# Sums of a graph-attention layer issued for two tiles at a time instead of three, a wait split over two accumulators, and four small operations given an earlier turn

## The chip, the cores and the metric

The kernel runs on one core of a Trainium2 chip. The metric is the device time of one execution in microseconds (us); of several runs the median is taken. A core has several engines, each of which works through its own list of instructions in order: TensorE (PE in the profile; PEld is its loading of weights) for matrix products and transposes, VectorE (DVE), ScalarE (ACT) and GpSimd (POOL) for elementwise work, and SyncE (SP), which here issues the transfers between memory and the core. [...]PE writes to PSUM, a small memory of accumulators, from which ACT or DVE must copy the results away ("evacuate" them) before the accumulator can be used again.

## The reference

The input is a graph with N = 3327 nodes, 256 features each, and a dense 3327 x 3327 matrix of edge weights, most of them zero. There are two layers, each of the form x = x + layer(relu(layernorm(x))).

Layer 0 runs two steps. In each, A is a sparsified attention matrix: logits q k^T over all pairs of nodes, softmax by row, and of each row the largest probabilities that together reach 0.9. R is the edge matrix plus identity, divided by its row sums.

```
for n in range(2):
    A  = top_p_attention(Xa, W1, W2, W3)      # 3327 x 3327
    Xf = R @ Xf
    Xa = A @ Xa
    Z  = Z + Xf @ U1[n].T + Xa @ U2[n].T
h = layernorm(X + Z) * g + b
```

Layer 1 is graph attention with four heads of 64 features:

```
e    = leaky_relu(s[:, :, None] + d[:, None, :], 0.2)   # per head, source i, neighbour j
e    = where(adj > 0, e, -inf)
attn = softmax(e over j)
out  = elu(attn @ hp)                                  # hp = h @ W, 64 features per head
```

The denominators of the last softmax are sums over j of the same exponentials that are multiplied with hp. They are the "sums" of this document.

## The kernel before

Nodes are split into 26 tiles of 128. The function that runs is `fast` (line 571).

**How the order comes about.** The kernel describes its work as pieces, each with an engine, an assumed length, a rank, the pieces it needs, and the buffers it takes and gives back (`put`). `Plan.order` (lines 470 to 567) then walks through an assumed time and gives each engine, whenever it is free, the piece of the lowest rank whose needs are met and whose buffers are free. The instructions are issued in exactly the order so found, so each engine's order is fixed in the program. A change of one rank or one buffer can therefore move pieces far away from it. The assumed lengths serve only to find the order; on the chip real durations count.

**Layer 0.** One row of the plan is a tile of 128 nodes against all 3327. There are 26 rows in each of two steps, 52 in all. For each row `search` (lines 1410 to 1458) finds the threshold above which probabilities are kept: logits on PE (L873), exponentials on ACT (L887), a first guess (`guess`, ACT), counts of what lies above the guess (`count`, ACT, L924, about 3.1 us each), a correction of the guess on POOL (`step`, lines 937 to 970), another count and step, in step 1 a third count with its step on DVE, then a search for the exact threshold on DVE (`window`, `sort`, `choose`) and the removal of everything below it (`drop`, L1034). `density` (lines 914 to 917) is four operations on one column of 128 values on ACT; its results are first read on POOL inside the first correction, that of L916 at L947 and that of L915 at L953. The first two counts of a row have rank -2.1 relative to the row, `density` -2.05: when both can go, the counts go first. `attention` (L1462) then transposes the row (PE L1047, copied by ACT L1052) and multiplies it with the features (PE L1059). `full` (L1477) holds the products of the edge matrix (PE L1091), which depend on no search and fill PE where a row isn't ready. At the end of a row small products and copies (L1227 to L1266) make the keys of the next step.

**Layer 1.** `attend_neighbours` (lines 1500 to 1811) goes over the 3327 target nodes in four quarters of W = 832 columns, and in each over 26 tiles of neighbours. Per tile:

- SP loads two blocks of the edge matrix, and ACT turns them into a mask of ones and zeros (L1623, L1624).
- DVE makes the exponentials times mask for four heads, two instructions of two heads each half (L1635), into an "e" buffer of the size 128 x 3328. The instructions' operand names vary: a tile uses one of four rotating buffers (pool "e") if its number modulo 7 is under 4, otherwise one of three fixed ones (shown as c and rhs in the profile; "e2" in the plan).
- PE multiplies the tile's features with the exponentials (L1651, `product`, two halves of two heads, each into its own accumulator of the PSUM pool "pl"; 8 records of the profile per half). One piece of the array is 128 x 64 there.
- PE adds the exponentials up over the neighbours (L1665, `sums`, 16 records per tile, in the accumulators acca and accf). One piece of the array is 128 x 32 there.

The sums of a tile are not issued with its products. They are gathered in a group of JG = 3 tiles, and each tile's sums give back its e buffer. After the last tile of a quarter, `leave` (lines 1707 to 1719) copies the two product accumulators (L1711, two instructions on ACT, one for each) and the sums (L1714) into one more buffer of the pool "e", called ot. From it, seven times, PE transposes 128 columns (L1732), DVE takes reciprocals (L1736), ACT makes the elu (L1744), DVE adds (L1748, L1749), and SP stores. This goes on while the next quarter's tiles already run. The last quarter ends with a different arrangement of the same work (lines 1767 to 1788).

The next quarter's first product needs both accumulators: it takes two "pl" buffers at once and needs the variable `evacuated`, the second of the two copies.

Of the kernel before, what the change touches and what calls it, by code (L numbers as in the profile page):

```python
# [10 lines left out]
F32 = mybir.dt.float32  # L11
# [8 lines left out]
P = 128  # L20
# [550 lines left out]
def fast(  # L571
# [59 lines left out]
    with ExitStack() as l0:  # L631
# [6 lines left out]
        ps_l = l0.enter_context(tc.tile_pool(name="ps_l", bufs=2, space=PSUM))  # L638
# [204 lines left out]
        plan = Plan(dict(rows=1, mvs=3, pl=2, px=2, acca=1, accf=1, accf0=1, accf1=1, et=3, at=4, y=1, e2=3, mask=2, **BUFS))  # L843
# [566 lines left out]
        def search(row, rank, keys, stats_of, fresh):  # L1410


            n, i = row.n, row.i
            got, a = [], None
            for g in range(2):

                def logits(g=g):
                    row.logits(2 * g)
                    row.logits(2 * g + 1)

                a = plan.put(
                    "PE", 2.1 - 0.7 * g, rank - 2.5, logits, needs=[keys, fresh, a], take=["pl", "pl"] + ["e", "sc"] * (1 - g)
                )
                for k in (2 * g, 2 * g + 1):
                    got.append(
                        plan.put("ACT", 1.15 if k < 3 else 0.5, rank - 2.5, row.exps, k, needs=[a], give=["pl"])
                    )
            row.pieces = dict(logits=a)
            a = plan.put("ACT", 0.35, rank - 2.4, row.row_sum, needs=[got])
            a = plan.put("POOL", 1.3, rank - 2.4, row.root, needs=[a, stats_of])  # L1430
            a = row.pieces["guess"] = plan.put("ACT", 1.0, rank - 2.4, row.guess, needs=[a])
            more = plan.put("ACT", 0.85, rank - 2.05, row.density, needs=[a])
            for j in range(2):
                got = [
                    plan.put("ACT", 3.05, rank - (2.1, 1.7)[j], row.count, j, fn, needs=[a])
                    for fn in (AF.Relu, AF.Sign)[j:]
                ]
                a = plan.put("POOL", (3.8, 4.7)[j], rank - (2.0, 1.6)[j], row.step, j, GP, needs=[got, more])
            if EVALS[n] == 3:
                a = row.pieces["counted"] = plan.put("ACT", 3.05, rank - 1.4, row.count, 2, AF.Sign, needs=[a])  # L1440
                a = plan.put("DVE", 2.7, rank - 1.3, row.step, 2, V, needs=[a])
            halves = []
            for h in range(2):
                for part in range(2):
                    a = plan.put(
                        "DVE", 3.2 - 2.0 * part, rank - 1.0, row.window, h, part, needs=[a], take=["y"] * (1 - part),
                        give=["y"] * part, lag=0.02, hold=1.95 * (1 - part),
                    )
                    halves.append(a)
            may = plan.put("POOL", 0.8, rank - 1.5, row.free, needs=[halves[2]])  # L1450
            a = plan.put("DVE", (1.8, 2.5)[n], rank - 1.0, row.sort, needs=[a])
            a = plan.put("DVE", 3.1, rank - 1.0, row.choose, needs=[a, may], take=["cum"])
            total = plan.put("POOL", 1.2, rank - 1.0, row.total, needs=[a], give=["cum"])
            drops = []
            for o in range(4):
                a = plan.put("DVE", 1.03, rank - 1.0, row.drop, o, needs=[a], hold=1.0)
                drops.append(a)
            return total, drops
# [41 lines left out]
        def attend_neighbours(rows, ends, done, fulls):  # L1500
# [1 line left out]

            W = NP // 4
            C = W // 2
            JG = 3
            logits_done = [r.pieces["logits"] for r in rows]
            freed = [p for p in done]
            extra = {}
# [23 lines left out]
            more = plan.put("SP", 0.02, 59.0, open_more, needs=[freed, opened], lag=0.0)  # L1532
# [41 lines left out]

            last, f_ = {}, None
            used_heads = [None, None]
            evacuated = None
            both = broadcast(0, 59.5)
            for b in range(4):
                lo = b * W  # L1580
                r0 = 60.0 + 10.0 * b
                q = {}
                tiles = range(lo // P, lo // P + 7)
                off = lo - tiles[0] * P

                def open_acc(q=q):
                    q["acc"] = [ps_l.tile([P, 2, 512], F32, name="pl") for _ in range(2)]

                def open_den(q=q):
                    q["den"] = [ps_a.tile([P, 512], F32, name=n) for n in ("acca", "accf")]  # L1590
# [1 line left out]
                seen, last_acc, last_den, last_e = [], None, None, None  # L1592
                group, groups_e = [], []
                for j in range(NT):
                    rank = r0 + 9.0 * j / NT
# [47 lines left out]

                    def product(a, j=j, held=held, q=q, open_acc=open_acc):

                        if j == 0 and a == 0:
                            open_acc()
                        for c in range(2):
                            for k in range(2):
                                h = 2 * a + k  # L1650
                                T.matmul(  # L1651
                                    q["acc"][a][k * FH : (k + 1) * FH, c, :C],
                                    main[:, j, h * FH : (h + 1) * FH],
                                    held["e"][:, h, c * C : (c + 1) * C],
                                    start=(j == 0),
                                    stop=(j == NT - 1),
                                )
# [20 lines left out]
                    else:  # L1678
# [6 lines left out]
                    x_ = plan.put(  # L1685
                        "DVE", 2.1, rank, exponents, 0, needs=[m_, both[0], ends[j][0], more if mine == "e2" else None,
                        logits_done, last_e], take=[mine], hold=2.0,
                    )
                    y_ = plan.put("DVE", 2.1, rank, exponents, 1, needs=[x_, both[1]], give=own, hold=2.0)
                    last_e = y_  # L1690
                    x_ = plan.put(
                        "PE", 1.42, rank, product, 0, needs=[x_, last_acc, evacuated], take=["pl", "pl"] * (j == 0)
                    )
                    last_acc = plan.put("PE", 1.42, rank, product, 1, needs=[x_, y_])
                    group.append((sums, mine))
                    if len(group) == JG or j == NT - 1:
                        for n_, (fn, name) in enumerate(group):
                            last_den = plan.put(
                                "PE", 1.42 + 0.2 * (n_ == 0), rank, fn, needs=[last_acc, last_den],
                                take=["acca", "accf"] * (j < JG and n_ == 0), give=[name],  # L1700
# [13 lines left out]
                            S.copy(q["ot"][:, 2, c], q["den"][c][:, :C])  # L1714

                r1 = r0 + 9.0
                evacuated = a = plan.put("ACT", 0.9, r1, leave, 0, needs=[last_acc], take=["e"], give=["pl"])
                evacuated = a = plan.put("ACT", 0.9, r1, leave, 1, needs=[a], give=["pl"])
                out_of = plan.put("ACT", 1.1, r1, leave, 2, needs=[a, last_den], give=["acca", "accf"])
                for x0 in range(0, W, P):  # L1720
                    m = min(P, W - x0, N - lo - x0)
# [74 lines left out]
                    elif x0 % (4 * P) == 0:  # L1796
                        f_ = plan.put("SP", 0.4, r1, fetch_all, needs=[used_heads[0] if x0 == 0 else [last_e, f_], touched], take=["e"] * (x0 > 0), lag=4.0)
                    a = plan.put(
                        "PE", 0.4, r1 + 0.02, turn, needs=[out_of], take=["px"], give=["e"] * (x0 + P >= W)
                    )  # L1800
                    if b == 3:
                        a = plan.put("DVE", 0.65, r1, quotient, needs=[a, f_], give=["px"])
# [27 lines left out]
        for n in range(STEPS):  # L1830
# [25 lines left out]
            if n == 0:  # L1856
# [25 lines left out]
                def layer1():  # L1882
# [8 lines left out]
                    give=["et", "et"],  # L1891
# [67 lines left out]
```

## Time and profile before

| | |
|---|---|
| three runs | 2218.48, 2219.33, 2220.72 us (median 2219.33) |
| profiled execution | 2222.8 us |
| its span | 2221.0 us |
| granted TensorE clock | 0.998 |
| PE busy | 2171.0 us in 11978 instructions |
| DVE, ACT, POOL busy | 1613.7, 1442.5, 931.3 us |
| L1651, products of layer 1, e buffers | 187.2 us, 1024 records of 515 ns |
| L1635, exponentials of layer 1, largest group | 128.6 us, 128 records of 1073 ns |
| L924, counts of layer 0 | 559.1 us, 182 records of 3072 ns |

In the rows of the profile an instruction is named by line, engine and operation, then what it writes and reads, with shapes; the numbers after it are the busy time of the group, the mean length of one in nanoseconds, and the idle time of the engine just before them with what ended it. Matrix products overlap in PE's pipeline, so the length of one record is longer than the pitch from one to the next. In a timeline, the first number is the start from the beginning of the span, the second the length of a run of equal instructions, and brackets give the idle time before it and what released it. Layer 1 takes about the last 480 us of the span; the quarters there begin some 119 us apart.

### The profile page before, as it was taken

Reading aid. Unit: us, or ns where it says so; the run is one execution under the profiler, and the core shown is the slowest. Engines: PE = TensorE matmul, PEld = TensorE weight load, DVE = VectorE, ACT = ScalarE, POOL = GpSimd, SP = SyncE. Lnnn points to the kernel's source line nnn. Section 1 sums busy time; section 2 is a strip of 40 time slices with the busy share of each in tenths; the row PEclk is TensorE's granted clock in tenths of the full one; section 3 lists DMA queues with packets and bytes.
Section 4 is the critical chain, followed back from the end, with each engine's and each line's share of the span. In section 5 each row is a group of like instructions: output and inputs, shape, how many; then the busy total and the mean of one; then the engine's idle time right before and its main releaser. Section 6 shows DMA issues by size and latency. Waiting matters only on the chain.

```text
span 2221.0 us, 35941 instructions
## 1 busy us (share of the span) xinstructions
PE 2171.0 (98%) x11978; PEld 1535.2 (69%) x11978; DVE 1613.7 (73%) x4229; ACT 1442.5 (65%) x2725; POOL 931.3 (42%) x2210
## 2 busy tenths in 40 slices
PE   7999999999999999999999999999999999999997
PEld 5388778777887788877878788887887433333333
DVE  5576656546655744277879877888777997989896
ACT  5766676567566661478888777878774455465553
POOL 5564455535544541256656666566653200000001
PEclk9999999999999999999999999999999999999999
DMA  4012121212212232622222222222225344444341
GB/s 120 1 45 80 52 71 54 71 52 62 71 54 71 71 91 67 189 82 60 63 58 63 62 72 74 80 62 64 67 77 152 117 130 143 116 137 126 107 127 50
DMA packets 192323, 183.75 MB, mean 83 GB/s; under 512 B 15386, under 2 KB 146176, under 8 KB 192128
## 3 DMA queue, kind: packets, MB, share of 16 engines
q1 hardware_dynamic: 190144, 180.10, 28.1%
q8 instruction: 96, 1.57, 0.3%
q10 hardware_dynamic: 1984, 1.26, 0.2%
q14 instruction: 99, 0.81, 0.1%
HBM read 164.41 MB, written 15.94 MB: 81 GB/s over the span
## 4 chain that ended last, share of the span: by engine, by line
PE 71%; issue 9%; ACT 8%; POOL 5%; DVE 5%; DMA 2%; SPq 0%; ACTq 0%; DVEq 0%; POOLq 0%
PE acca L1059 20%; PE accf L1091 20%; PE pl L1651 9%; PE pl L873 6%; ACT junk L924 6%; PE px L1047 6%; PE acca L1665 2%; PE accf L1665 2%; PE px L1258 2%; PE px L1209 1%; PE px L1354 1%; POOL sc L937 1%; ACT et L1052 1%; DVE e L1635 1%; PE px L1236 1%
## 5 line engine op out<-in xcount | busy, mean ns | idle before, releaser
L1059 PE MATMUL acca<-rhs,et 128*128 128x256 f32 x2704 | 620.7, 380 | 1.7 <-ACT et L1052 1.6
L924 ACT ACTIVATE junk<-e,sc 128x3327 fp8e5<-128x3327 f32 x182 | 559.1, 3072 | 48.0 <-POOL sc L969 46.6
L1059 PEld LDWEIGHTS acca<-rhs,et 128*128 128x128 f32 x2704 | 499.4, 191 | 66.0 <-ACT et L1052 4.8
L1091 PE MATMUL accf<-c,at 128*128 128x256 f32 x1352 | 313.5, 382 | 6.1 <-ACT f L1098 6.1
L1091 PE MATMUL accf<-main,at 128*128 128x257 f32 x1352 | 310.3, 381 | 3.0 <-DMA at<-in_adjt_dram 2.8
L979 DVE SCALAR_TENSOR_TENSOR y<-e,sc 128x1664 f32<-128x1664 f32 x104 | 208.1, 2001 | 127.1 <-POOL sc L966 125.1
L1052 ACT COPY et<-px 128x512 f32<-128x512 f32 (+1 forms) x364 | 192.6, 553 | 142.0 <-PE acca L1059 83.4
L1091 PEld LDWEIGHTS accf<-c,at 128*128 128x128 f32 x1352 | 250.0, 190 | 48.3 <-ACT f L1098 10.9
L1091 PEld LDWEIGHTS accf<-main,at 128*128 128x128 f32 x1352 | 251.0, 190 | 44.9 <-issue 6.5
L984 DVE MAX8 cands<-y 128x8 f32<-128x208 f32 x832 | 242.4, 361 | 3.6
L1034 DVE SCALAR_TENSOR_TENSOR e<-e,thr 128x832 f32<-128x832 f32 x208 | 212.9, 1079 | 2.0
L887 ACT ACTIVATE e<-pl 128x1024 f32<-128x1024 f32 x208 | 179.0, 863 | 37.6 <-PE pl L873 36.9
L1624 ACT ACTIVATE et<-at 128x448 bf16<-128x448 f32 (+1 forms) x204 | 112.3, 550 | 137.4 <-DVE e L1635 81.6
L1047 PE MATMUL px<-ident,e 128*128 128x128 f32 x1352 | 191.4, 274 | 7.1 <-ACT et L1052 2.3
L1784 POOL TENSOR_TENSOR qq<-qq 128x256 f32<-128x256 f32 x4 | 3.0, 755 | 453.7 <-ACT qq L1780 453.7
L1047 PEld LDWEIGHTS px<-ident,e 128*128 128x128 f32 x1352 | 160.1, 141 | 47.0 <-issue 11.8
L1651 PE MATMUL pl<-e,main 128*64 128x416 f32 x1024 | 187.2, 515 | 0.0
L873 PE MATMUL pl<-kt,qq 64*128 64x512 f32 (+1 forms) x832 | 173.5, 535 | 0.0
L1651 PEld LDWEIGHTS pl<-e,main 128*64 128x64 f32 x1024 | 71.1, 137 | 107.3 <-issue 91.9
L1635 DVE SCALAR_TENSOR_TENSOR e<-c,low,et 128x832 f32<-128x832 f32 x128 | 128.6, 1073 | 7.9 <-PE accf L1665 3.6
L873 PEld LDWEIGHTS pl<-kt,qq 64*128 64x128 f32 x832 | 71.6, 186 | 83.9 <-issue 77.9
L1635 DVE SCALAR_TENSOR_TENSOR e<-qq,low,et 128x832 f32<-128x832 f32 x120 | 120.4, 1076 | 2.6 <-ACT e L1711 2.0
(527 smaller groups left out, 3083.9 us busy)
## 6 DMA issues: line engine op xcount, KB each, us to landing
at<-in_adjt_dram SPq DMA_DIRECT2D x414, 256.0 KB
at<-in_adjt_dram SPq DMA_DIRECT2D x102, 192.0 KB
at<-in_adjt_dram SPq DMA_DIRECT2D x52, 128.0 KB
ys<-ystage SPq DMA_DIRECT2D x26, 256.0 KB
rhs<-in_x_dram SPq DMA_DIRECT2D x26, 128.0 KB
ystage<-in_x_dram SPq DMA_DIRECT2D x26, 128.0 KB
base<-ys SPq DMA_DIRECT2D x26, 128.0 KB
x1s<-ystage SPq DMA_DIRECT2D x26, 128.0 KB
```

The source lines that it names most:

```text
L873: T.matmul(pl[:, r, :m], qq[half, self.i, :], kt[half, 512 * k : 512 * k + m], start=True, stop=True,)
L887: S.activation(self.e[:, 1024 * k : 1024 * k + 2 * w].rearrange("p (r w) -> p r w", r=2), pl, AF.Exp, accum_out=(self.p0, self.p1, self.p2 ...
L924: S.activation(junk[:, :N], self.e[:, :N], fn, bias=t, scale=-1.0, accum_out=dst, saturate=False)
L979: V.scalar_tensor_tensor(self.y[:, : hi - lo], self.e[:, lo:hi], self.up, self.e[:, lo:hi], ALU.is_lt, ALU.mult, accum_out=(self.h0, self. ...
L984: V.max(self.cands[:, o // PIECE, :], self.y[:, o - lo : min(o + PIECE, hi) - lo])
L1034: V.scalar_tensor_tensor(piece, piece, self.thr[:, o : o + 1], piece, ALU.is_gt, ALU.mult)
L1047: T.transpose(pt[:, k, :], self.e[:, j * P : (j + 1) * P], ident)
L1052: S.copy(self.et[g][:, :m, :], self.pt.pop(g)[:, :m, :])
L1059: T.matmul(self.acc, et[:, j - 4 * g, :], rhs[self.n][:, j, :], start=(j == 0), stop=(j == NT - 1))
L1091: T.matmul(self.acc[:, : self.w], self.at[j // JC][:, j % JC, :], self.src[:, j, : self.w], start=(j == 0), stop=(j == NT - 1),)
L1635: V.scalar_tensor_tensor(held["e"][:, k, :], extra["both"][b % 2][:, k, :], low[:, j, k : k + 1], held["mask"], ALU.max, ALU.mult,)
L1651: T.matmul(q["acc"][a][k * FH : (k + 1) * FH, c, :C], main[:, j, h * FH : (h + 1) * FH], held["e"][:, h, c * C : (c + 1) * C], start=(j == 0),
```

## The change

Three edits. The size of a group of sums, JG, goes from 3 to 2. The two product accumulators of a quarter are opened one at a time: the first half product takes one "pl" buffer and waits for the first copy, the second half product takes the other and waits for the second copy. And `density` gets the rank -2.2, lower than that of the row's first two counts, so that the plan issues it ahead of them when both can go.

```diff
--- before.py
+++ after.py
@@ -1429,7 +1429,7 @@
             a = plan.put("ACT", 0.35, rank - 2.4, row.row_sum, needs=[got])
             a = plan.put("POOL", 1.3, rank - 2.4, row.root, needs=[a, stats_of])
             a = row.pieces["guess"] = plan.put("ACT", 1.0, rank - 2.4, row.guess, needs=[a])
-            more = plan.put("ACT", 0.85, rank - 2.05, row.density, needs=[a])
+            more = plan.put("ACT", 0.85, rank - 2.2, row.density, needs=[a])
             for j in range(2):
                 got = [
                     plan.put("ACT", 3.05, rank - (2.1, 1.7)[j], row.count, j, fn, needs=[a])
@@ -1502,7 +1502,7 @@
 
             W = NP // 4
             C = W // 2
-            JG = 3
+            JG = 2
             logits_done = [r.pieces["logits"] for r in rows]
             freed = [p for p in done]
             extra = {}
@@ -1574,17 +1574,17 @@
 
             last, f_ = {}, None
             used_heads = [None, None]
-            evacuated = None
+            evacuated = [None, None]
             both = broadcast(0, 59.5)
             for b in range(4):
                 lo = b * W
                 r0 = 60.0 + 10.0 * b
-                q = {}
+                q = {"acc": {}}
                 tiles = range(lo // P, lo // P + 7)
                 off = lo - tiles[0] * P
 
-                def open_acc(q=q):
-                    q["acc"] = [ps_l.tile([P, 2, 512], F32, name="pl") for _ in range(2)]
+                def open_acc(a, q=q):
+                    q["acc"][a] = ps_l.tile([P, 2, 512], F32, name="pl")
 
                 def open_den(q=q):
                     q["den"] = [ps_a.tile([P, 512], F32, name=n) for n in ("acca", "accf")]
@@ -1643,8 +1643,8 @@
 
                     def product(a, j=j, held=held, q=q, open_acc=open_acc):
 
-                        if j == 0 and a == 0:
-                            open_acc()
+                        if j == 0:
+                            open_acc(a)
                         for c in range(2):
                             for k in range(2):
                                 h = 2 * a + k
@@ -1689,9 +1689,11 @@
                     y_ = plan.put("DVE", 2.1, rank, exponents, 1, needs=[x_, both[1]], give=own, hold=2.0)
                     last_e = y_
                     x_ = plan.put(
-                        "PE", 1.42, rank, product, 0, needs=[x_, last_acc, evacuated], take=["pl", "pl"] * (j == 0)
+                        "PE", 1.42, rank, product, 0, needs=[x_, last_acc, evacuated[0]], take=["pl"] * (j == 0)
                     )
-                    last_acc = plan.put("PE", 1.42, rank, product, 1, needs=[x_, y_])
+                    last_acc = plan.put(
+                        "PE", 1.42, rank, product, 1, needs=[x_, y_, evacuated[1]], take=["pl"] * (j == 0)
+                    )
                     group.append((sums, mine))
                     if len(group) == JG or j == NT - 1:
                         for n_, (fn, name) in enumerate(group):
@@ -1714,8 +1716,9 @@
                             S.copy(q["ot"][:, 2, c], q["den"][c][:, :C])
 
                 r1 = r0 + 9.0
-                evacuated = a = plan.put("ACT", 0.9, r1, leave, 0, needs=[last_acc], take=["e"], give=["pl"])
-                evacuated = a = plan.put("ACT", 0.9, r1, leave, 1, needs=[a], give=["pl"])
+                first = plan.put("ACT", 0.9, r1, leave, 0, needs=[last_acc], take=["e"], give=["pl"])
+                a = plan.put("ACT", 0.9, r1, leave, 1, needs=[first], give=["pl"])
+                evacuated = [first, a]
                 out_of = plan.put("ACT", 1.1, r1, leave, 2, needs=[a, last_den], give=["acca", "accf"])
                 for x0 in range(0, W, P):
                     m = min(P, W - x0, N - lo - x0)
```

## The prediction, made before the changed kernel had run

> **What bounds the kernel now.** I read the shares of busy time, then the chain that ended last, then the groups with shapes kept apart, then the waits, and last the timelines of TensorE (PE), VectorE (DVE) and GpSimd (POOL) at the places where layer 1 goes from one quarter to the next and where a row's search starts.
>
> ```profile
> PE 2171.0 (98%) x11978; PEld 1535.2 (69%) x11978; DVE 1613.7 (73%) x4229; ACT 1442.5 (65%) x2725; POOL 931.3 (42%) x2210
> ...
> PE 71%; issue 9%; ACT 8%; POOL 5%; DVE 5%; DMA 2%; SPq 0%; ACTq 0%; DVEq 0%; POOLq 0%
> ```
>
> PE is busy for nearly the whole span of 2221.0 us. No edit takes a product away, so only PE's idle stretches, its slower stretches, and what the edits add to it can move the end.
>
> ```profile
> L1665 PE MATMUL acca<-e,qd 128*32 128x416 f32 x512 | 57.0, 517 | 0.0
> ...
> L1651 PE MATMUL pl<-e,main 128*64 128x416 f32 x1024 | 187.2, 515 | 0.0
> ...
> L914 ACT ACTIVATE sc<-sc 128x1 f32<-128x1 f32 x52 | 10.8, 207 | 0.0
> ```
>
> Products use 128x64 pieces of the array, sums 128x32 ones. Density is four ACTIVATE like the last row: 207, 203, 186, 187 ns (0.78 us).
>
> ```profile
> DVE e L1635 <- PE accf L1665: 4.2, 4, 2.0
> DVE e L1635 <- ACT e L1711: 4.0, 2, 2.0
> PE pl L1651 <- DVE rhs L1635: 1.9, 5, 1.0
> POOL sc L947 <- ACT sc L917: 9.1, 13, 1.8
> POOL sc L947 <- ACT sc L916: 5.1, 7, 1.1
> ```
>
> The first two are DVE waiting for an e buffer that the sums have not given back yet, or that the evacuation's tile holds; the third is what PE shows of it; the last two are POOL's step standing for density.
>
> Timelines around the change from quarter 0 to 1, PE first, then DVE, then ACT:
>
> ```profile
> 1839.23 3.01 PE L1651 MATMUL pl<-e,main 128*64 128x416 f32 x16
> ...
> 1847.90 3.01 PE L1651 MATMUL pl<-e,main 128*64 128x416 f32 x16
> ...
> 1872.64 4.60 PE L1651 MATMUL pl<-rhs,main 128*64 128x416 f32 x16 [1.03 <-DVE rhs L1635]
> ...
> 1881.50 3.01 PE L1651 MATMUL pl<-rhs,main 128*64 128x416 f32 x16
> ```
> ```profile
> 1846.71 4.07 DVE L1635 SCALAR_TENSOR_TENSOR e<-c,low,et 128x832 f32<-128x832 f32 x4 [2.02 <-PE accf L1665]
> ...
> 1860.16 2.08 DVE L1635 SCALAR_TENSOR_TENSOR e<-c,low,et 128x832 f32<-128x832 f32 x2 [1.31 <-PE accf L1665]
> ```
> ```profile
> 1845.09 0.85 ACT L1711 COPY e<-pl 128x832 f32<-128x832 f32 x1 [0.54 <-PE pl L1651]
> ```
>
> From tile 24's products (1839.23) to tile 6's (1881.50) PE takes 42.27 us. The same stretch takes 41.70 at each of the next two changes (1958.65 to 2000.35, 2077.50 to 2119.20). Its work without waits: 8 tiles of products at 2.79, 8 of sums at 1.40, 21 transposes and six to nine changes of shape, together about 38.3. So some 4.0 and twice 3.4 us are waits, in part dissolved in groups that the trace shows as long ones (4.60 for 16 records, where 3.01 is usual). Their origin is on DVE: it stands 2.02 and 1.31 us for sums, the short reciprocals and adds of the old quarter come in between, and it never recovers the lead.
>
> **What the Trainium skill says.** "TensorEngine Tiling (Array Packing)", Key Properties: changing the tiling mode, not just the tile, drains TensorE. The trace agrees and prices it: three tiles take 12.857 us (products at 1894.43, 1907.28, 1920.14), 36 pairs at the undisturbed pitch of 0.349 would take 12.56, so about 0.29 for a group of sums with its two changes. "Perfetto Trace Analysis", Identifying Performance Opportunities: a gap that repeats can mean too few buffers for the next tile; the same loss at all three quarter changes agrees. "TensorE: Matmul & The Clock Gate", Architectural detail: ACT and DVE take instructions strictly in order; so what is put ahead of a count on ACT delays it by its whole length.
>
> **Part 1, groups of two.** Before, a quarter's 26 tiles make 9 groups, after 13; four quarters give 16 more groups at 0.29, **+4.7 us** on PE. A middle tile costs PE 4.33 instead of 4.286. DVE's two halves of two instructions cost 4.0 a tile, so PE remains the slower there and pays all of it. If only the two slower pitches seen at changes count (0.442 against 0.349 each), it is 16 x 0.19 = 3.0; that is the low end, 4.7 the high one and my value.
>
> The gain: a group's sums hand back its e buffers. Tile 3 of a new quarter takes the buffer of tile 0, which the sums of tiles 0 to 2 free (DVE's 1860.16); after, the sums of 0 and 1 do, issued ahead of tile 2's products, some 4 us earlier. The evacuation's own e tile and tile 2 likewise get theirs from groups that end sooner. Writing the new order beside the old durations, DVE's waits at the first change nearly vanish, and PE keeps about 1.25 (fifth and seventh tile, behind the old quarter's reciprocals and adds, 0.17 to 0.43 us each, which nothing moves): 4.0 to 1.25, **-2.75**. At the other two, 3.4 to about 1.1, **-2.3** each. Together -7.4 (bounds: -9 if another 1.6 of what remains goes as well, -3 if DVE's small work is the true limit). What is late next is DVE itself, with about 4.0 a tile plus 6.7 of boundary work against PE's 38.3.
>
> Sum of part 1: +4.7 - 7.4 = **-2.7 us**.
>
> **Part 2, split of the wait.** The second half product may run into its own accumulator once that alone is evacuated. In the trace both evacuations are done by 1845.94, while the old quarter's sums keep PE until 1847.8: the first product waits for neither. After, the e tile that the evacuation needs comes later by up to the length of a group, and the evacuations reach about the moment of use; the split keeps this from costing. I take **0**; -0.3 to +0.5 per change if ACT's masks (0.58 each) go ahead of it. The cover is those sums, 2.8 us; without it, it would cost up to two copies, 1.7, per change.
>
> **Part 3, density ahead of the counts.** No instruction is added. In all 52 rows four tiny ACT operations, about 0.78 to 0.85 us, move ahead of both counts (3.07 each); in most rows they stood behind one to three evacuation copies (0.37 to 0.58 each). POOL's step at L947 loses a wait of 23.2 us in all, 0.45 a row, and gets its counts 0.8 later: a row's latency changes by +0.35 on average, between -1 and +0.85. In the middle of layer 0 PE has adjacency products as filler, so this is hidden. It shows where a row is the only thing left: the first row (there POOL stands 1.04 at 67.73, so about neutral: 0, -0.2 to +0.8), the first row of step 1 (+0.75 at most, I take +0.4), and the last row of step 0. At that last one, the third count starts at 826.24, behind copies of another row on ACT; PE then idles 2.35 us at 853. The new order has counts back to back, and puts products of the attention between the small matrix products where adjacency products stood: I take half of the 2.35, -1.2 (0 to -2.4). The end of layer 0 has an exponent half fewer between two windows on DVE, but six adjacency products (2.6 us) left at the end: 0, +-2. The ranks also shift the whole order of adjacency products by a place or two: 0, +-2. Sum of part 3: **-0.8**.
>
> **Sum.** -2.7 + 0 - 0.8 = -3.5 us on the profiled execution: span 2217.5, with the 1.8 around it 2219.3 beside its 2222.8. The runs' median lies 3.5 below that execution, so I set 2219.33 - 3.5 = **2215.8**. A difference of 0.2% (4.4 us) is about the smallest that a measurement here tells from none.
>
> **Rivals.** *More is freed* (0.25). The boundary waits go down to nothing (-9.7) at the low switch price (+3.0), and the idle at 853 and part of the other gaps of layer 0 (some 19 us after the start) are filled: -6.7 - 2.5 = about 2210. For it: PE idles only because things come late, and both edits bring things earlier. Against it: DVE's boundary work is not moved.
>
> *DVE sets the boundary, not its buffers* (0.12). Then the earlier buffers buy nothing at three changes, and 16 groups at 0.29 are paid in full: +4.7, with +0.4 at step 1's start, 2224.4. Slower. For it: DVE's small work fills much of 1851 to 1876, and PE's last wait there is on DVE and not on a buffer. Against it: 3.3 us of DVE's delay are explicitly waits for sums. It decides if a change gains less than 0.1 us.
>
> *Density costs what it moves* (0.18). Counts 0.85 late on the first rows of both steps and the last, and an order of layer 0 that fits PE less well, cost 3 to 4 us and eat the gain: about 2219.5, no change. For it: ACT is 8% and POOL 5% of the chain. Against it: those waits of POOL are taken away.
>
> *The split does nothing* is part of my forecast; if it does more, it adds to the first rival.
>
> **Numbers.** My case has 0.45, with 2213 to 2218.5 as its own range; two fifths of it lie under 2214.9. The first rival is faster throughout. So faster 0.18 + 0.26 = 0.44, same 0.27 + 0.15 = 0.42, slower 0.14 (all of the second rival and a little of the third). The range 2209 to 2224 leaves out the outer parts of the first and second rivals.
>
> **What would show it.** Right: 52 groups of sums; stretches from tile 24 to tile 6 of about 39.5; DVE's waits for accf at L1635 well under 4.2; middle pitch near 4.33 a tile; POOL's wait for density at L947 gone; the start of quarter 0 as early as before, give or take 2 us. Wrong: stretches still above 41 (the second rival), a middle pitch far from 4.33, or layer 1 starting several us off, which would put the cause in layer 0's order.

## The result, and the profile after

The changed kernel takes 2209.87 us (median of 5 runs, 2209.17 to 2210.82); the kernel before, run beside it, 2220.72. The ratio is 0.9951, with a 95% interval from 0.994 to 0.9962: 10.9 us faster, and at least 8.4. The forecast was 2215.8 with a range from 2209 to 2224. The time lies in the range, near its lower end, and on the side that had the larger chance; the gain is three times the 3.5 us of the forecast.

The page's line of busy times, after:

```profile
PE 2168.2 (98%) x11978; PEld 1529.5 (69%) x11978; DVE 1614.2 (73%) x4229; ACT 1443.1 (65%) x2725; POOL 932.3 (42%) x2210
```

Each engine's count of instructions is the same. The span fell from 2221.0 to 2208.1, PE's busy time from 2171.0 to 2168.2 only: what went is nearly all time in which PE stood. Of the groups with shapes kept apart, those that answer to the ones shown of before:

```profile
L1665 PE MATMUL acca<-e,qd 128*32 128x416 f32 x512 | 57.3, 519 | 0.0
...
L1651 PE MATMUL pl<-e,main 128*64 128x416 f32 x1024 | 191.3, 517 | 0.2
...
L914 ACT ACTIVATE sc<-sc 128x1 f32<-128x1 f32 x52 | 10.1, 194 | 0.0
```

And of the waits (engine, what it wrote, line, what it waited for; us in all, times, longest):

```profile
POOL sc L941 <- ACT junk L924: 154.4, 42, 8.6
...
DVE e L1635 <- PE accf L1665: 11.5, 3, 4.4
...
DVE e L1635 <- ACT e L1713: 3.3, 2, 1.7
```

PE's waits for DVE's exponents in layer 1 (L1651 after rhs, 1.9) and POOL's for density (L947, 9.1 and 5.1) are gone from the list. POOL now stands longer for the counts: 154.4 us at L941, where it was 109.4. And DVE now waits 11.5 us for buffers that the sums hand back, more than the 4.2 of before.

PE's timeline at the change from quarter 0 to 1, then DVE's there and at the next change:

```profile
1830.71 3.01 PE L1651 MATMUL pl<-e,main 128*64 128x416 f32 x16
...
1839.38 3.01 PE L1651 MATMUL pl<-e,main 128*64 128x416 f32 x16
...
1863.31 3.86 PE L1651 MATMUL pl<-rhs,main 128*64 128x416 f32 x16
...
1870.04 3.01 PE L1651 MATMUL pl<-rhs,main 128*64 128x416 f32 x16
```
```profile
1848.84 4.04 DVE L1635 SCALAR_TENSOR_TENSOR e<-c,low,et 128x832 f32<-128x832 f32 x4
...
1965.21 2.08 DVE L1635 SCALAR_TENSOR_TENSOR e<-qq,low,et 128x832 f32<-128x832 f32 x2 [4.38 <-PE accf L1665]
```

From tile 24 to tile 6 PE takes 39.33 us instead of 42.27. Of PE's waits one is left, inside the 3.86 that stands where 3.01 is usual. Tile 3's exponents start 18.1 us after tile 24's products (1848.84 against 1830.71), before 20.9 (1860.16 against 1839.23). The wait of 4.38 is no loss: DVE is early there. At the same change before, the small work of the old quarter came first and tile 3's exponents started 20.3 us after tile 24's products (1978.95 against 1958.65); after, 17.1 (1965.21 against 1948.12), and the small work follows.

**Where the 12.9 us of the two traces are.** Both traces were cut at the same pieces of work on PE: its first product, the last attention product of chosen rows of layer 0 (L1059, 52 records a row), tile 24 of each quarter, and its last record. Where one kernel has done more adjacency products by then than the other, 0.432 us are taken off for each pair of records. Differences to the one trace of the kernel before, in us, for this change and for the experiments told below; the last column is their sum, and the stars are explained under the table:

| kernel | start to first product | to row 25 of step 0 | row 26, the last of step 0 | rows 1 to 9 of step 1 | rows 10 to 24 | from there to tile 24 of quarter 0 | three quarter periods and end | sum |
|---|---|---|---|---|---|---|---|---|
| the change | -1.25 | -1.36 | -4.02 | -0.54 | +0.07 | -1.41 | -4.36 | -12.88 |
| groups_only | -0.97 | -0.49 | +0.01* | +0.23 | -0.03 | +0.99 | -4.43 | -4.71 |
| density_only | -1.10 | +0.12* | -4.02 | -0.56 | -0.06 | -2.69 | +0.02 | -8.28 |
| new_order_late | -1.05 | +0.09* | -4.02 | +5.65** | +0.77 | -2.69 | +0.01 | -1.23 |
| old_order_early | -0.78 | +9.20*** | +0.03* | +2.46 | +4.73 | +0.06 | +0.02 | +15.71 |
| density_last0 | -0.48 | +0.26 | -3.32 | +0.30 | -0.04 | -0.17 | +0.03 | -3.42 |
| density_lasts | -0.93 | +0.41 | -3.28 | +0.56 | +0.10 | -2.55 | +0.04 | -5.63 |
| split_only | -1.02 | -0.11 | -1.67 | +0.19 | -0.03 | +1.37* | +3.47 | +2.19 |
| no_split | -0.72 | +0.45 | -4.02 | -0.38 | +0.12 | -1.41 | -4.44 | -10.41 |
| middle_two | -0.83 | -0.14 | -1.67 | +0.18 | -0.02 | -0.85 | +4.94 | +1.61 |
| edges_222 | -1.49 | +0.46 | -4.02 | -0.38 | +0.12 | -2.41 | -3.41 | -11.14 |
| late_threes | -0.53 | -1.05 | -4.02 | +0.04 | -0.02 | -2.40 | -5.99 | -13.98 |
| ones | -1.14 | -0.94 | -1.68 | +0.11 | 0.00 | +4.08 | +2.98 | +3.42 |

Two columns must be read with care. The first is chance: every kernel starts its first product 0.5 to 1.5 us earlier than the one profiled execution of before (10.76 us), whatever its edit; the second scatters by up to 1.8 us between kernels whose order there is the same (density_only, no_split, edges_222, late_threes and the change).

The stars stand for TensorE's clock. While PE works, the granted clock in these traces is 1.0 from about 20 us on, but for a few stretches of 3.41 us at 0.5. Each costs some 1.7 us, and each star is one in that kernel's trace; the two of new_order_late follow each other. The trace of before has one as well, in the last row of step 0. There the same eight products of the attention (L1059) took 3.53 us in before and 1.89 in split_only, whose order is the same at this place. The two stretches, with the granted clock as the third number from the end:

```profile
858.44:861.97 3.53, 3.53 (x12) 2.76 (x11) 0.00 (x0) 0.58 (x1) 0.00 (x0) 0.53 0.00 0
```
```profile
857.27:859.16 1.89, 1.89 (x12) 1.64 (x11) 0.00 (x0) 0.59 (x1) 0.00 (x0) 1.00 0.00 0
```

So groups_only and old_order_early, which have such a stretch there too, show about 0 in this column, and split_only, middle_two and ones, which have none, -1.67. Of the -4.02, then, some 2.35 are idle time of PE that the new order fills, and 1.67 are a stretch of half the clock, which three traces with the old order have there and three do not.

Without the first column 11.6 us are left. Some 4.4 are in layer 1's periods, 4.0 at the last row of step 0, of which 1.7 are the clock, and 1.4 where layer 0 goes over to layer 1: the 2.7 of density_only, less about 1.2 for four further groups in quarter 0. The other 1.8 lie in the column that scatters and in step 1.

### The profile page after: what moved, and what is told of

The parts are those of the page before. It is cut to its first block, busy times and chain, and to the rows that moved or that the text cites. A ratio compares the mean times of both kernels' runs of the same rounds, so it can differ in the third digit from the quotient of the medians.

```text
span 2208.1 us, 35934 instructions
## 1 busy us (share of the span) xinstructions
PE 2168.2 (98%) x11978; PEld 1529.5 (69%) x11978; DVE 1614.2 (73%) x4229; ACT 1443.1 (65%) x2725; POOL 932.3 (42%) x2210
## 5 line engine op out<-in xcount | busy, mean ns | idle before, releaser
L1059 PE MATMUL acca<-rhs,et 128*128 128x256 f32 x2704 | 616.8, 379 | 0.0
L1059 PEld LDWEIGHTS acca<-rhs,et 128*128 128x128 f32 x2704 | 499.3, 190 | 62.5 <-issue 1.5
L1034 DVE SCALAR_TENSOR_TENSOR e<-e,thr 128x832 f32<-128x832 f32 x208 | 213.1, 1080 | 1.8
L1651 PE MATMUL pl<-e,main 128*64 128x416 f32 x1024 | 191.3, 517 | 0.2
L1651 PEld LDWEIGHTS pl<-e,main 128*64 128x64 f32 x1024 | 70.8, 137 | 112.2 <-issue 87.3
L1635 DVE SCALAR_TENSOR_TENSOR e<-c,low,et 128x832 f32<-128x832 f32 x128 | 128.5, 1072 | 8.8 <-PE accf L1665 7.1
L1635 DVE SCALAR_TENSOR_TENSOR e<-qq,low,et 128x832 f32<-128x832 f32 x120 | 120.5, 1076 | 6.0 <-PE accf L1665 4.4
```

Of the source, the lines that this page charges most:

```text
L1034: V.scalar_tensor_tensor(piece, piece, self.thr[:, o : o + 1], piece, ALU.is_gt, ALU.mult)
L1059: T.matmul(self.acc, et[:, j - 4 * g, :], rhs[self.n][:, j, :], start=(j == 0), stop=(j == NT - 1))
L1635: V.scalar_tensor_tensor(held["e"][:, k, :], extra["both"][b % 2][:, k, :], low[:, j, k : k + 1], held["mask"], ALU.max, ALU.mult,)
L1651: T.matmul(q["acc"][a][k * FH : (k + 1) * FH, c, :C], main[:, j, h * FH : (h + 1) * FH], held["e"][:, h, c * C : (c + 1) * C], start=(j == 0),
```

## The experiments

Each time stands beside that of the kernel before, run together with it; the median of before lies between 2220.05 and 2222.64 us.

**Each large part alone.** Groups of two, and density's rank, each as the only edit.

```diff
-            JG = 3
+            JG = 2
```

> Before with groups of two tiles alone. Theory A (the gain of layer 1 is buffers handed back sooner, less the price of 16 more groups): about -3 us in all; from tile 24's to the next tile 24's products 119.4, 118.9, 118.9 becomes 117.4, 117.7, 117.7; layer 0 as before. Theory B (the groups bring nothing by themselves, all of the gain is layer 0's): +3 to +5 us. Theory C (the groups bring most of the 11 us): -8 or more.

2218.59 us against 2221.04, ratio 0.9987 (0.998 to 0.9994), -2.5 us. The periods from tile 24 to tile 24 are 117.41, 117.64 and 117.64, where before has 119.42, 118.85 and 118.85; layer 0 is as before. Theory A holds, B and C fall.

```diff
-            more = plan.put("ACT", 0.85, rank - 2.05, row.density, needs=[a])
+            more = plan.put("ACT", 0.85, rank - 2.2, row.density, needs=[a])
```

> Before with density ahead of the counts alone. Theory A: about -7 us, nearly all up to the last row of layer 0 (some 4 us at the end of step 0, the rest at the end of layer 0 and in step 1), layer 1's quarter periods unchanged at 118.9. Theory C: -2 us or less. My written forecast had -0.8.

2215.91 against 2221.04, 0.9979 (0.997 to 0.9987), -5.1 us; in the table -4.02 at the last row of step 0, or -2.35 without the clock, and -2.69 at the way into layer 1. Theory A has the places right; its 7 us have the clock in them. The larger part of the whole gain is density's. The two medians add up to -7.6, short of -10.9 by about what the three intervals allow; from the last row of step 0 on, the pieces of the traces add up: -3.2 and -7.3 for the change's -10.3.

**Is it the order, or POOL's shorter wait?** The new rank does two things: POOL no longer stands for density, and the plan finds another order for thousands of pieces. Two kernels separate them. In one the plan is that of density_only, but the four instructions are issued right behind the second count; in the other the plan is that of before, but they are issued right behind the guess. The pieces where they stood remain in the plan, and issue nothing.

```diff
-            more = plan.put("ACT", 0.85, rank - 2.2, row.density, needs=[a])
+            more = plan.put("ACT", 0.85, rank - 2.2, (lambda: None), needs=[a])
...
-                    plan.put("ACT", 3.05, rank - (2.1, 1.7)[j], row.count, j, fn, needs=[a])
+                    plan.put("ACT", 3.05, rank - (2.1, 1.7)[j], (lambda j=j, fn=fn: (row.count(j, fn), row.density() if (j, fn) == (0, AF.Sign) else None)), needs=[a])
```

> The order of density_only on every engine, except that density's four instructions stand right behind the second count on ACT instead of ahead of the first. Theory O (the gain of layer 0 comes from the order of the other pieces that the new rank leads to): nearly as fast as density_only, within 2 us of it. Theory L (the gain comes from POOL no longer waiting for density, so that the row's own chain is shorter): back to the time before, within 2 us, or slower.

2219.91 against 2221.04, 0.9996 (0.9988 to 1.0005): no difference from before, and 4.0 us slower than density_only. By the total, theory L; by the table, O at the two places that matter: -4.02 and -2.69 are there to the hundredth. POOL's wait for density, though, did not come back as was meant: no wait at L947 is in the list, and the first operation of the correction, L941, starts 0.10 us (median) behind the end of a count, as in density_only. So this kernel tests density's place on ACT, not POOL's wait. What is lost is elsewhere: +5.65 in the first nine rows of step 1, nearly all of it at one place. PE's waits for the copies in this kernel, then PE at that place, in this kernel and in density_only:

```profile
PE px L1047 <- ACT et L1052: 5.9, 5, 3.3
```
```profile
1092.44 1.97 PE L1047 MATMUL px<-ident,e 128*128 128x128 f32 x8 [3.31 <-ACT et L1052]
```
```profile
1089.58 1.14 PE L1047 MATMUL px<-ident,e 128*128 128x128 f32 x8 [0.54 <-ACT et L1052]
```

And ACT at the same place, first in this kernel, then in density_only:

```profile
1088.76 3.07 ACT L924 ACTIVATE junk<-e,sc 128x3327 fp8e5<-128x3327 f32 x1 [4.66 <-POOL sc L969]
...
1091.82 1.05 ACT L1052 COPY et<-px 128x512 f32<-128x512 f32 x2
```
```profile
1085.90 3.07 ACT L924 ACTIVATE junk<-e,sc 128x3327 fp8e5<-128x3327 f32 x1 [1.37 <-POOL sc L969]
```

A row's count waits 4.66 us for POOL's step. The copy that frees PE's next transposes belongs to another row and needs none of this, but it stands behind that count on ACT, and PE stands with it, 2.8 us longer than in density_only. In the middle of PE's wait two stretches of half the clock begin, one behind the other (the eight transposes take 1.97 us for 1.14); they are the other 3.4 us. POOL does not wait for density here. It works without a pause from 1079.41 to 1088.72, but the operations of the step's end are long, first in this kernel, then in density_only:

```profile
1084.42 0.94 POOL L963 TENSOR_TENSOR sc<-sc 128x1 f32<-128x1 f32 x1
...
1086.46 2.26 POOL L969 TENSOR_SCALAR sc<-sc 128x1 f32<-128x1 f32 x1
```
```profile
1084.34 0.19 POOL L963 TENSOR_TENSOR sc<-sc 128x1 f32<-128x1 f32 x1
...
1084.90 0.96 POOL L969 TENSOR_SCALAR sc<-sc 128x1 f32<-128x1 f32 x1
```

They run while DVE removes the small probabilities of another row (L1034), from 1084.23 on here and from 1084.60 on there, where L963 is over by then. So at this place a shift of less than half a microsecond between two engines made the loss, and ACT's queue carried it to PE. That it falls so in every execution is not shown; the 4.0 us between the two medians say that something of this size does.

```diff
-            a = row.pieces["guess"] = plan.put("ACT", 1.0, rank - 2.4, row.guess, needs=[a])
-            more = plan.put("ACT", 0.85, rank - 2.05, row.density, needs=[a])
+            a = row.pieces["guess"] = plan.put("ACT", 1.0, rank - 2.4, (lambda: (row.guess(), row.density())), needs=[a])
+            more = plan.put("ACT", 0.85, rank - 2.05, (lambda: None), needs=[a])
```

> The order of before on every engine, except that density's four instructions stand right behind the guess on ACT. Theory O: the time of before, within 2 us, since the order of the other pieces is the old one. Theory L: as fast as density_only, within 2 us.

2233.11 against 2221.04, 1.0054 (1.0041 to 1.0068): 12 us slower. Neither theory foresaw it. The table's +15.71 comes from its slowest execution (2238.17), and three stretches of half the clock make 5.1 of it. The rest is spread over all of layer 0 (some 4.1 up to row 25, +2.5, +4.7), and part of it shows in the same wait, here in the old order with density early:

```profile
PE px L1047 <- ACT et L1052: 5.5, 10, 1.4
```

Before had 2.3 in 4 waits there. The counts come some 0.8 us later, and so do the copies that stand behind them on ACT; that this makes all of the loss is argued, not shown. POOL's waits for density are gone in this kernel, and it is slower: the gain is not POOL's shorter wait. An order that was made for density late pays for density early in many rows; one made for density early does not. O and L both fall as they were put: at the ends of the steps the order gives the gain by itself, in the other rows order and place must fit.

**In which rows?** Density ahead in the last row of step 0 alone, then in the last row of both steps; all other rows keep -2.05.

```diff
-            more = plan.put("ACT", 0.85, rank - 2.05, row.density, needs=[a])
+            more = plan.put("ACT", 0.85, rank - (2.2 if (n, i) == (0, NT - 1) else 2.05), row.density, needs=[a])
```

> Before with density ahead of the counts in one row of 52 only, the last of step 0. Its order differs from before's at that row alone. Theory R (the gain of density is a gain at the ends of the two steps): -4 us, all of it between the attention of rows 25 and 26 of step 0, where PE's waits of 2.08 and 1.64 us go, and nothing elsewhere. Rival (it is spread over the rows): within 1 us of before.

2218.84 against 2220.05, 0.9993 (0.9986 to 1.0), -1.2 us; in the trace -3.32, all at the row named, of which 1.67 are the clock in the trace of before. R holds in the place; its size, 4, is too high. PE at that place, before and then in this kernel:

```profile
857.93 0.72 PE L1047 MATMUL px<-ident,e 128*128 128x128 f32 x4 [2.08 <-DVE gk L783]
858.44 3.53 PE L1059 MATMUL acca<-rhs,et 128*128 128x256 f32 x8
```
```profile
854.00 1.89 PE L1059 MATMUL acca<-rhs,et 128*128 128x256 f32 x8
...
855.90 0.60 PE L1047 MATMUL px<-ident,e 128*128 128x128 f32 x4
```

The expectation took the long record of 3.53 us for a second wait, of 1.64; it is the stretch of half the clock. Here products of the row stand in the gap, and neither the wait of 2.08 nor the stretch is there.

```diff
-            more = plan.put("ACT", 0.85, rank - 2.05, row.density, needs=[a])
+            more = plan.put("ACT", 0.85, rank - (2.2 if i == NT - 1 else 2.05), row.density, needs=[a])
```

> Before with density ahead of the counts in two rows, the last of each step. Theory R: -7 to -8 us in the trace, 4 at the end of step 0 and 3.6 where layer 0 goes over to layer 1, that is as much as moving it in all 52 rows. Rival: less than half of that.

2216.36 against 2220.05, 0.9981 (0.9972 to 0.999), -3.7 us, beside -5.1 for all 52 rows. In the trace -3.28 and -2.55 at the two ends, no gain in between. PE at the end of layer 0, before and then in this kernel:

```profile
1706.79 10.63 PE L1091 MATMUL accf<-c,at 128*128 128x256 f32 x48 [1.77 <-ACT f L1098]
...
1720.62 0.87 PE L1047 MATMUL px<-ident,e 128*128 128x128 f32 x6 [0.85 <-DVE e L1034]
```
```profile
1702.34 8.90 PE L1091 MATMUL accf<-c,at 128*128 128x256 f32 x40 [0.46 <-ACT f L1098]
```

Waits of 2.62 us become 0.46, which is most of the 2.55. Two rows of 52 make most of density's gain, which is Theory R in the place; its 7 to 8 us had the clock in them too.

**The split of the wait.** Alone, then taken out of the changed kernel.

```diff
-                        "PE", 1.42, rank, product, 0, needs=[x_, last_acc, evacuated], take=["pl", "pl"] * (j == 0)
+                        "PE", 1.42, rank, product, 0, needs=[x_, last_acc, evacuated[0]], take=["pl"] * (j == 0)
...
-                    last_acc = plan.put("PE", 1.42, rank, product, 1, needs=[x_, y_])
+                    last_acc = plan.put(
+                        "PE", 1.42, rank, product, 1, needs=[x_, y_, evacuated[1]], take=["pl"] * (j == 0)
```

> Before with the split of the wait over the two accumulators alone. Theory A: 0, within 1 us, as both copies are done 2 us before the next quarter's first product. Rival: a gain of 2 us or more, since the two edits run alone so far make -7.6 of the -10.9.

2224.89 against 2222.64, 1.0011 (1.0002 to 1.002): 2.3 us slower. The second and third change cost 1.72 us more each (43.43 us from tile 24 to tile 6 for 41.71); the +1.37 on the way to quarter 0 comes from a stretch of half the clock. The timelines of DVE and PE in this kernel:

```profile
1985.11 0.18 DVE L1739 RECIPROCAL mv<-px 128x4 f32<-128x4 f32 x1 [1.60 <-PE px L1735]
```
```profile
1986.32 2.61 PE L1651 MATMUL pl<-c,main 128*64 128x416 f32 x8 [1.24 <-DVE c L1635]
```

The order has changed: two reciprocals of the old quarter now stand ahead of tile 4's exponents on DVE, where before the second stood between their halves. The likely reason is that the first product is free a little sooner in the plan's time. The second reciprocal waits 1.60 us for PE's transposes, the exponents behind it with it, and PE waits for those.

```diff
-                        "PE", 1.42, rank, product, 0, needs=[x_, last_acc, evacuated[0]], take=["pl"] * (j == 0)
+                        "PE", 1.42, rank, product, 0, needs=[x_, last_acc, evacuated], take=["pl", "pl"] * (j == 0)
...
-                        "PE", 1.42, rank, product, 1, needs=[x_, y_, evacuated[1]], take=["pl"] * (j == 0)
+                        "PE", 1.42, rank, product, 1, needs=[x_, y_]
```

> Groups of two and density ahead, without the split of the wait. Theory A: as fast as the changed kernel, within 1 us, about 2210. Rival (the split is needed for the earlier buffers to pay, as the evacuation comes later with groups of two): 2 to 4 us slower than the changed kernel, about 2213; the stretch from tile 24's to tile 6's products then above 39.3, 38.4, 38.4.

2212.8 against 2222.64, 0.996 (0.9946 to 0.9973), -9.8 us, beside the changed kernel's 0.9951. All of layer 1 is the changed kernel's: -1.41 and -4.44 for -1.41 and -4.36. With groups of two the split shows no worth; the rival falls.

**Where in a quarter do groups of two pay?** First in the middle alone, then at the changes alone. Both replace the fixed size by a list.

```diff
-            JG = 3
+            SIZES = [3] * 2 + [2] * 7 + [3] * 2
+            LAST = [sum(SIZES[: k + 1]) - 1 for k in range(len(SIZES))]
...
-                    if len(group) == JG or j == NT - 1:
+                    if j in LAST:
```

> Before with groups of two only in the middle of a quarter (sizes 3, 3, seven times 2, 3, 3; 11 groups for 9). Theory A (gain at the quarter changes, price in the middle): no gain, 8 more groups at 0.29 make +2.3 us; stretches from tile 24 to tile 6 at 42.3, 41.7, 41.7 or longer (a last group of three instead of two). Rival (shorter groups help everywhere): faster than before by 1 us or more.

2226.04 against 2222.64, 1.0018 (1.001 to 1.0027), 3.4 us slower. The periods grow by 0.58, 1.50 and 1.50, and the stretches from tile 24 to tile 6 are 43.6, 44.0 and 44.0. The first figure is the price of two further groups, 0.29 each; the rest came with a last group of three. That is Theory A. The -0.85 on the way to quarter 0, where two further groups should add 0.6, is not explained.

```diff
-            JG = 2
+            SIZES = [2] * 3 + [3] * 6 + [2]
```

> The changed kernel with groups of two only at the quarter changes (sizes 2, 2, 2, six times 3, 2; 10 groups for 13). Theory A: the stretches from tile 24 to tile 6 stay within 0.5 of 39.3, 38.4, 38.4, and 12 fewer groups at 0.29 save 3.5 us: about 2206.5. Rival (the middle's early buffers are needed too): no faster than the changed kernel.

2211.35 against 2222.64, 0.9954 (0.994 to 0.9967), -11.3 us, no clear difference from the changed kernel, as the rival has it. The stretches at the changes are indeed 39.3, 38.4 and 38.4, so three groups of two at the start of a quarter make all of the gain there. But the periods are 117.73, 117.97 and 118.00 where three fewer groups should leave each 0.9 under the changed kernel's 117.41, 117.67 and 117.67. The first group of three behind the change:

```profile
1873.66 7.02 PE L1652 MATMUL pl<-e,main 128*64 128x416 f32 x32
```

5.81 us is usual for 32 records: 1.2 us of wait. Three tiles in a row take PE 2.79 each and DVE 4.0 each, so a group of three needs exponents made ahead, and right after a change DVE has none.

**A version that uses this.** Quarter 0 with threes first and twos at its end, the others with twos until DVE has its lead, then threes.

```diff
-            JG = 2
...
+                SIZES = [3] * 6 + [2] * 4 if b == 0 else [2] * 6 + [3] * 4 + [2]
+                LAST = [sum(SIZES[: k + 1]) - 1 for k in range(len(SIZES))]
```

> The changed kernel with groups of three where DVE has its lead back: quarter 0 in six threes and four twos, the other quarters in six twos, four threes and a two (10 and 11 groups for 13). Theory A with the condition that edges_222 pointed to (a group of three costs a wait only while DVE has no lead, and it gains about 0.3 us a tile with groups of two): periods from tile 24 to tile 24 of 117.1 for 117.7, and 0.9 off quarter 0; about 2.5 us faster than the changed kernel, 2207.5. Rival (a group of three costs a wait wherever it stands): no faster than the changed kernel.

2207.83 against 2220.05, 0.9943 (0.993 to 0.9957), -12.2 us. The periods are 116.83, 117.21 and 117.09, 0.5 to 0.6 under the changed kernel's, and the way to tile 24 of quarter 0 is 1.0 shorter. It is the fastest kernel here by its median and in every period; by the ratios the intervals of the two overlap.

**Smaller still.** Sums after every tile.

```diff
-            JG = 3
+            JG = 1
```

> Before with sums after every tile (26 groups a quarter for 9). Theory A (0.29 us for every further group, and nothing more to gain at the quarter changes than groups of two gain): 13 groups more than groups of two make +3.8 a quarter, periods from tile 24 to tile 24 of about 121.4 against groups_only's 117.4 to 117.6, in all some 12 us slower than before, 2232. Rival (a shorter group goes on paying through earlier buffers): periods under 119.

2227.79 against 2220.33, 1.0031 (1.0021 to 1.0042), 7.5 us slower, where 12 were expected. In the middle of a quarter a tile takes 4.478 us, against 4.334 with twos and 4.286 with threes: half a group more costs 0.144, a sixth 0.048, so a group costs 0.29 at every size. The periods are 120.04, 119.88 and 119.89, not 121.4: at the changes four more groups should add 1.16, and 39.4, 39.3 and 39.3 for 39.3, 38.4 and 38.4 is 0.1 to 0.9 more. Smaller groups do buy a little more there, and not what they cost.

## Why the prediction was right, and where it was wrong

The range held the time and the sign was right, but with some luck. The time lies outside the main case's own range, 2213 to 2218.5, and the kernel before was 1.4 us slower beside the changed one than where the forecast started (2220.72 for 2219.33): the ratio taken of 2219.33 is 2208.5, just under the range. Part 1 came about as forecast; what was missed is nearly all in Part 3.

**Part 1** was right, in sign and size. The price of a group, 0.29, is 0.31 in quarter 1 after the change (78.08 for 77.15 us from tile 6 to tile 24, three groups more). The stretches of "about 39.5" are 39.3, 38.4 and 38.4; part of the last two is given back from tile 6 on, and the three periods together gave 4.4 us, where the step's -2.75, -2.3 and -2.3 with four further groups in each period make 3.9. What is late next was named rightly, too: in edges_222 it is DVE that makes PE wait. The sign of success was read wrongly: "DVE's waits for accf at L1635 well under 4.2" are 11.5. The gain is that DVE's next exponents start earlier; how long DVE stood before them says nothing, as its small work merely moved from before the wait to behind it.

**Part 2** was right for this change: nothing, with the sums as cover. Its bound was not. "-0.3 to +0.5 per change" was reasoned from the wait and its cover; alone, the split costs 1.72 at two changes, by an order in which a reciprocal that waits stands ahead of exponents. That such an edit can lead the plan to a different order was not foreseen.

**Part 3** failed in size: -0.8 was said, -5.1 measured for density alone. Two terms of the sum were too small. For the last row of step 0 the idle time of 2.35 was taken and halved; the new order fills all of it, and in the trace of before 1.67 more went with the stretch of half the clock behind it. The end of layer 0 was put at 0, within 2, because an exponent half fewer and six products left over were set against each other; PE's waits there went from 2.62 to 0.46 us, and the stretch gave -2.6 to -2.7 (density_lasts, density_only). The first row of step 1, +0.4, shows no loss: -0.56 over nine rows. The 23.2 us at L947 were read too high: 14.2 of them were waits for density, and 10.7 us of short idle times are still there after. And the sentence "PE has adjacency products as filler, so this is hidden" was true of the new order only: old_order_early moves density just as far and loses 12 us. The prediction cited that ACT works strictly in order, and drew from it only what a count loses, not what the copies behind the count lose. new_order_late shows how such a loss gets to PE, in a case where the count itself stands for POOL.

**The rivals.** "More is freed", 2210, has the right time for partly the wrong reasons: its layer 0 gaps were filled, but switches kept their full price. The stretches came down to 38.4 at two changes, against the 38.3 of PE's bare work, but 1.2 us of that is given back behind tile 6, and the first stretch stays at 39.3. "DVE sets the boundary" fell with groups_only. "Density costs what it moves" fell too, though old_order_early shows what it would have looked like.

## What to carry to other kernels

In a kernel whose order a planner finds, a rank is worth what the order is worth that it leads to: price the ends of stages, where nothing is left to fill with, by all of the bound engine's idle time, and list what stands behind the moved piece on its engine. Where a record is long, look at the granted clock before calling it a wait. To tell the order from the operation's own place, issue the operation at its old place within the new order, and the reverse. Smaller groups that return buffers early belong where the producer has lost its lead, and larger ones where it has it back.

## What the runs showed of the hardware that was not expected

The price of a change of array shape, from 128x64 to 128x32 and back, was the same 0.29 us with groups of one, two and three tiles, so it can be worked out once and multiplied.

A wait of PE can cost more than its length. The stretches of half the clock in the fourteen traces while PE worked, ten if the double one of new_order_late counts as one, all begin inside a wait of PE of 1.85 us or more, or within 1.3 us of its end. Other waits as long had none behind them, such as the 2.10 us that ended at 856.81 in split_only. What decides it is not shown.

Small operations on POOL are slower while DVE runs L1034. In the trace of before, L960 takes 0.84 us (median) in the 8 cases that lie mostly within one, and 0.19 in the other 96.

PE's first product started between 9.3 and 10.8 us into the span in kernels with the same beginning, a scatter of 1.5 us beside the 2.5 that groups of two bring; two single traces should be compared from that product on.
